# The last graph layer in eight units of 128 queries, its GpSimd operations as queued items of their own, and the folding of weights behind a step's piece

## The chip, the cores and the metric

The kernel runs on one core of a Trainium2 chip. The metric is the device time of one execution in microseconds (us), from runs on the chip; the profile of one execution gives start and length of every instruction on TensorE (PE, with its weight loads as PEld), VectorE (DVE), ScalarE (ACT), GpSimd (POOL) and the queue that issues most DMAs (SP).

## What is computed

Sixteen graphs of 1024 nodes with 128 features share one adjacency matrix. Three layers of masked attention with eight heads, each followed by a feed-forward network with layer norms, come first. Then comes one last layer of additive attention. Cut to what matters:

```python
# layers 0, 1, 2, for h [16, 1024, 128]; 8 heads of 16
scores = einsum('bnhd,bmhd->bhnm', Q, K) / sqrt(16)
scores = where(adj == 0, -inf, scores)
x = layer_norm(h + softmax(scores) @ V @ Wo + bo, ln1)
x = layer_norm(x + relu(x @ W1 + b1) @ W2 + b2, ln2)

# the last layer
h = x @ W
s_i = h @ a_src
s_j = h @ a_dst
e = s_i[:, :, None] + s_j[:, None, :]
e = where(e >= 0, e, 0.2 * e)
e = where(adj == 0, -inf, e)
y = softmax(e) @ h + x
return layer_norm(y, ln_gamma, ln_beta)
```

The kernel uses that exp(leaky(e)) is exp(0.2 s_i) exp(0.2 s_j) max(1, exp(0.8 (s_i + s_j))). The first factor cancels in the softmax, the second is multiplied into the node rows (`hd`), and what is left, max(1, product) times the 0/1 mask, is an outer product of two vectors of exponentials: that is what `edges` builds.

## The kernel before

**Blocks and steps.** A block m is one attention layer of one graph; there are 48. Four graphs ("lanes") go together: block order is layer 0 of graphs 0 to 3, layer 1 of graphs 0 to 3, layer 2 of them, and then the next four graphs. A block has 32 steps (g, qh, kt): two groups of four heads, two halves of 512 queries, eight tiles of 128 keys. So there are 1536 steps in a row, and n counts them. A half of a block here means the eight steps of one (g, qh).

**A step.** `score_step` (L532) issues four float32r matmuls of 512 columns (L540), the scores S of four heads, into two PSUM tiles from `slot()` (ring "s" of three). Of the first two heads, ACT takes the exponential (L548) and POOL multiplies by the 0/1 mask (L549); in eleven of the 32 steps (`BOTH_ON_DVE`), and always for the other two heads, DVE adds the mask (L552) and ACT takes the exponential after it (L564). The result is an `e_tile()`, from a ring of six. `av_due(n)` then issues the AV matmuls (L569) of the step four before (`AHEAD` = 4), which accumulate over eight steps; after the eighth DVE transposes the accumulator (L580) and POOL scales it (L584).

**Pieces.** All other work is cut into tasks that lie in chains. A task is (gap, function, tiles): it is due when its gap in steps since the chain's last task is over, and the tile words say which shared buffers it takes or frees. `piece()` (L863) runs after a step's AV and takes at most one due task without a star, and any number with a star. When a block ends its chains get the rest of its layer (attention output, feed-forward), and after layer 2 of a graph the tasks of the last layer, `last_tasks(b)` (L696). `need(mark)` forces a chain to its end at once if something later cannot start without it. A graph's x sits in one of five "x" tiles from its load until the task `store` frees it ("-x"); the load of graph b + 4's x needs such a tile, and its transpose by PE (L340) starts in the block ahead of its own.

**The last layer, for one graph.** xt(0) and xt(1) transpose x; xt(1) also lets POOL scale and shift x by the second layer norm of layer 2 (`scale_shift`, L440 and L441, 1024 elements wide). Three `nodes` tasks project (L378 with `w_nodes`) and take the exponentials. `rows_gh` and `send_rows` turn the two vectors of exponentials into rows and send them by 16 small DMAs to `g_rows` and `h_rows`, split into high and low parts, so that each edge matmul contracts four rows. Then four units u of 256 queries follow: `edges(u)` issues, for two slots, four float32r matmuls of 256 columns each (L772) in two row groups, and eight DVE operations of 128x256 that take the maximum with 1 and multiply by the mask (STT, L776) into an e tile; `aggregate(u)` issues the matmuls of that tile with `hd` (L378, tile `t<-hd,e`), then reciprocal (L789), scale and add x (L792), and statistics on DVE; after each second unit `normalise` runs on POOL (three small operations, then four at L436). `end` is four 512-wide operations on POOL by ln_gamma and ln_beta, and `store` eight DMAs (L811).

**Who orders what.** PE, ACT and SP execute in the order in which the program issues. DVE and POOL are ordered by a scheduler, by priority; `tc.issue_after(behind["pool"])` pins an instruction behind the newest mask multiply on POOL, and `soon()` raises a priority.

**Setup.** The dictionary `setup` (L316) holds, by step number, the loading and folding of later layers' weights (steps 8 to 82). Its matmuls (L273, L280, L291, L307) are issued ahead of the scores of their step:

```python
                now[0] = n
                if at == (6 if m == 0 else 1):
                    stack(m, 1)
                for run in setup.get(n, ()):
                    run()
```

Of the kernel before, what the change touches and what calls it, by code (L numbers as in the profile page):

```python
# [9 lines left out]
F32 = mybir.dt.float32  # L10
F32R = mybir.dt.float32r
BF16 = mybir.dt.bfloat16
# [6 lines left out]
P = 128  # L19
# [3 lines left out]
J = 4  # L23
# [96 lines left out]
def fast_path(ctx: ExitStack, tc: tile.TileContext, a: dict, out: bass.AP, flag):  # L120
# [28 lines left out]
        return work.tile([P, 512], F32, tag="w", name=name, bufs=TILES["w"])  # L149

    def e_tile():
        return work.tile([P, J, 512], F32, tag="e", name="e", bufs=6)


    def tokens(v):
# [36 lines left out]
    mask_add = const.tile([P, NT, N], F8W)  # L192
    rows_in = []
    for t in range(NT):
        if t < 6:
            ai = work.tile([P, 2, N], I32, tag="e", name="ai", bufs=6)
            ai, ab = ai[:, 0], ai.bitcast(BF16)[:, 1, :N]
        else:
# [497 lines left out]
    def last_tasks(b):  # L696
        s = {}
        g0 = 32 * (b % 2)

        def xt(h):  # L700
            def run():
                w = W[L - 1]
                if h == 0:

                    s["col"] = work.tile([P, 4, NT], F32, tag="col", name="col", bufs=2)
                    s["hd"] = [work.tile([P, 4, D + 1], F32, tag="w", name="hd", bufs=TILES["w"]) for _ in range(2)]
                    s["n"] = with_stats(state["x", b])
                s["xT", h] = half_tile("xT")
                transpose_half(s["xT", h], state["x", b], h, w["ln2_gc"], w["ln2_bc"])
                if h == 1:  # L710
                    scale_shift(state["x", b], w["ln2_g"], ln2_b_last)
            return run

        def nodes(t0, t1):
            def run():
                col, ts = s["col"], slice(t0, t1)

                halves = [slice(max(t0, 4 * h), min(t1, 4 * h + 4)) for h in range(2)]
                halves = [(c, s["hd"][c.start // 4][:, c.start % 4:(c.stop - 1) % 4 + 1, :])
                          for c in halves if c.start < c.stop]  # L720
# [36 lines left out]

        def edges(u):
            def run():
                e = s["e", u] = e_tile().rearrange("p j (c q) -> p (j c) q", q=256)  # L760
                half = slice(u // 2 * 512, u // 2 * 512 + 512)

                def queries(v):
                    return v.rearrange("p (j q) -> p j q", j=4)[..., u % 2 * 64:u % 2 * 64 + 64]

                for c in range(2):

                    ps = slot()
                    for i in range(2):
                        for r in range(2):  # L770
                            row = slice(64 * r + g0, 64 * r + g0 + 4)
                            nc.tensor.matmul(ps[:, (2 * r + i) * 256:(2 * r + i + 1) * 256],  # L772
                                             h_rows[row, (2 * i + c) * P:(2 * i + c + 1) * P],
                                             queries(g_rows[row, half]), start=True, stop=True)
                    for i in range(4):
                        nc.vector.scalar_tensor_tensor(e[:, c + 2 * i, :], ps[:, i * 256:(i + 1) * 256], 1.0,  # L776
                                                       queries(mask01[:, c + 2 * i, half]), op0=OP.max, op1=OP.mult)
            return run

        def aggregate(u):  # L780
            def run():
                e, ps = s["e", u], bank()
                for i in range(2):
                    for t in range(NT):
                        by_columns(ps[:, i * (D + 1):(i + 1) * (D + 1)],
                                   e[:, t, :].rearrange("p (j i e) -> p i j e", j=4, i=2)[:, i],
                                   s["hd"][t // 4][:, t % 4, :], start=(t == 0), stop=(t == NT - 1))
                pv = ps[:, :2 * (D + 1)].rearrange("p (i d) -> p i d", d=D + 1)
                nc.vector.reciprocal(s["col"][:, 3, 2 * u:2 * u + 2], pv[:, :, D])  # L789
                for i in range(2):  # L790
                    t = 2 * u + i
                    nc.vector.scalar_tensor_tensor(s["n"][0][:, t, :], pv[:, i, :D], s["col"][:, 3, t:t + 1],  # L792
                                                   state["x", b][:, t, :], op0=OP.mult, op1=OP.add)
                stats(s["n"], slice(2 * u, 2 * u + 2))
                if u % 2:
                    normalise(s["n"], slice(2 * u - 2, 2 * u + 2))
                if u == 3:
                    check_range(s["col"].rearrange("p c t -> p (c t)"))
            return run

        def end():
            y = s["n"][0]
            for h in range(2):
                scale_shift(y[:, 4 * h:4 * h + 4, :], wl["ln_gamma"], wl["ln_beta"])

        def store():
            y = s["n"][0]
            for h in range(2):
                queue = nc.scalar if h and b == B - 1 else nc.sync
                for j in range(4):  # L810
                    queue.dma_start(tokens(out[b])[j][:, h], y[j * SLOT:(j + 1) * SLOT, 4 * h:4 * h + 4, :])  # L811

        def two(f, g):
            def run():
                f()
                g()
            return run

        return [(5, xt(0), "+w +last +w +w"), (1, xt(1), "+w"), (2, nodes(0, 3), ""), (2, nodes(3, 6), ""), (2, nodes(6, 8), "-w -w"),
                (2, rows_gh, ""), (1, send_rows, "*"), (7, edges(0), ""), (3, two(edges(1), aggregate(0)), ""),  # L820
                (3, two(edges(2), aggregate(1)), ""), (3, two(edges(3), aggregate(2)), ""),
                (3, aggregate(3), ""), (4, end, "-last -w -w *"), (5, store, "-x *")]

    blocks = [(b, l) for p in range(0, B, LANES) for l in range(L) for b in range(p, p + LANES)]
# [121 lines left out]
    with tc.manual_schedule(engines={mybir.EngineType.PE, mybir.EngineType.Activation, mybir.EngineType.SP}):  # L949
        for m, (b, l) in enumerate(blocks):  # L950
# [284 lines left out]
```

## Time and profile before

| | |
|---|---|
| three runs | 3985.82, 3988.66, 3991.97 us; median 3988.66 |
| the profiled execution | 3988.0 us, its span 3985.9 us |
| mean granted TensorE clock | 0.975 |
| busy share of the span | PE 94%, DVE 87%, POOL 85%, ACT 83% |
| an ordinary block (3 to 8, 16 to 21, 28 to 33, 40 to 45 nearly all) | 70.9 us |
| blocks 10 to 15 | 82.2, 100.9, 100.3, 97.3, 96.1, 70.3 us |
| blocks 22 to 27 | 82.1, 101.1, 97.9, 96.8, 96.1, 70.4 us |
| blocks 34 to 39 | 82.7, 100.6, 100.3, 97.4, 96.0, 70.4 us |
| blocks 1 and 2 (weights are folded) | 73.5, 84.1 us |
| blocks 46 and 47 | 89.2, 99.6 us |
| from the end of block 47 to the end | 115 us |

A block's length is the time between the ends of its last accumulator transpose (L580) and that of the block before. The span runs from the first to the last instruction; the time of the execution holds 2.1 us more. In the windows below a line has the stretch, its length, then for each engine its busy time with the number of instructions, then the granted clock, the DMA engines' busy share and GB/s. A line of a timeline has start, length, engine, source line, operation, result<-operands, shape and count; in brackets the idle time ahead of it and what ended it. A line of waits has engine and waiting line, the line that it waited for, us in total, number of times and the longest. A line of groups has the busy total, the mean ns of one, and the idle time before. L378 and L340 are the lines of helpers, so these instructions are told apart by their tiles.

### The profile page before, as it was taken

How to read it: one execution, taken by the hardware profiler on the slowest of the kernel's cores; microseconds unless marked ns; L12 is line 12 of the kernel's file. 1: busy time of each engine (PE TensorE's matmuls, PEld its weight loads, DVE VectorE, ACT ScalarE, POOL GpSimd, SP SyncE). 2: the span in 40 equal slices, each digit the busy share in tenths (PEclk: the TensorE clock that was granted, in tenths of full speed). 3: DMA queues.
4: the chain of work that ended last, by engine and by line, in shares of the span. 5: the costliest groups of instructions: out<-in, count | busy, mean ns of one | idle time of the engine just before them, and what ended most of it. 6: DMA issues, size and time to landing. Idle time of an engine off the chain costs nothing.

```text
span 3985.9 us, 108397 instructions
## 1 busy us (share of the span) xinstructions
PE 3735.5 (94%) x43873; PEld 1501.6 (38%) x43873; DVE 3480.8 (87%) x5844; ACT 3289.4 (83%) x3797; POOL 3393.9 (85%) x2923
## 2 busy tenths in 40 slices
PE   7999999999999999998999999999999999999887
PEld 2333333344433333334444333333444433333346
DVE  6889999988889999998888999998888899999765
ACT  7989999977778999996776999998767799999750
POOL 4889999977789999997778999998778899999784
PEclk8999999999999999999999999999999999999998
DMA  5423424322223424332222423333222333324100
GB/s 139 114 65 92 100 71 111 80 66 65 66 66 87 111 69 104 84 90 67 62 67 68 112 67 102 88 85 98 66 55 66 86 75 99 94 73 115 49 7 20
DMA packets 245880, 319.19 MB, mean 80 GB/s; under 512 B 51072, under 2 KB 174208, under 8 KB 245376
## 3 DMA queue, kind: packets, MB, share of 16 engines
q1 hardware_dynamic: 243840, 311.52, 31.3%
q8 instruction: 349, 5.72, 0.6%
q14 instruction: 155, 1.27, 0.1%
q10 hardware_dynamic: 1536, 0.68, 0.1%
HBM read 58.53 MB, written 51.38 MB: 28 GB/s over the span
## 4 chain that ended last, share of the span: by engine, by line
PE 44%; DVE 23%; ACT 10%; POOL 8%; issue 6%; SPq 2%; DMA 1%; ACTq 0%; DVEq 0%; POOLq 0%
PE acc L569 16%; DVE e L552 16%; PE t L378 14%; PE s L540 11%; ACT e L564 5%; ACT e L548 3%; POOL e L549 2%; ACT hT L644 2%; POOL x L436 2%; PE s L378 1%; POOL x L440 1%; DVE st L408 1%; POOL x L441 1%; POOL mv L430 1%; DVE aT L598 1%
## 5 line engine op out<-in xcount | busy, mean ns | idle before, releaser
L552 DVE TENSOR_TENSOR e<-s,mask_add 128x1024 f32<-128x1024 f32 x2064 | 2410.6, 1209 | 166.7 <-PE s L540 133.6
L549 POOL TENSOR_TENSOR e<-e,mask 128x1024 f32<-128x1024 f32 x1008 | 2030.6, 2029 | 436.3 <-ACT e L548 435.5
L564 ACT ACTIVATE e<-e 128x1024 f32<-128x1024 f32 x2064 | 2145.0, 1061 | 190.6 <-DVE e L552 171.6
L569 PE MATMUL acc<-e,v 128*17 128x512 f32 x12288 | 1641.5, 606 | 52.2 <-POOL e L549 48.1
L540 PE MATMUL s<-Wq,Wk 64*128 64x512 f32 x6144 | 1237.7, 464 | 84.6 <-ACT e L548 29.8
L548 ACT ACTIVATE e<-s 128x1024 f32<-128x1024 f32 x1008 | 1032.2, 1024 | 311.7 <-PE s L540 311.0
L540 PEld LDWEIGHTS s<-Wq,Wk 64*128 64x128 f32 x6144 | 509.0, 186 | 1218.4 <-DVE e L552 492.6
L569 PEld LDWEIGHTS acc<-e,v 128*17 128x17 f32 x12288 | 205.6, 95 | 552.3 <-issue 418.4
L436 POOL TENSOR_SCALAR x<-x,mv 128x128 f32<-128x128 f32 x896 | 391.3, 453 | 19.2
L430 POOL TENSOR_TENSOR mv<-mv,half_neg 128x4 f32<-128x4 f32 (+1 forms) x179 | 214.3, 1197 | 14.7
L415 DVE TENSOR_TENSOR x<-t,x 128x512 f32<-128x512 f32 x191 | 132.0, 691 | 106.0 <-PE t L378 102.4
L378 PE MATMUL t<-x1T,W 128*32 128x512 f32 x1520 | 200.8, 600 | 5.1 <-DVE parts L743 3.2
L408 DVE BATCH_NORM_STATS2 st<-x 128x6 f32<-128x128 f32 x896 | 198.1, 281 | 6.3
L378 PEld LDWEIGHTS t<-W,hT 128*32 128x32 f32 x6080 | 173.8, 112 | 63.9 <-issue 57.0
L378 PE MATMUL t<-hd,e 128*32 128x129 f32 x6656 | 194.9, 274 | 3.0 <-DVE lo L468 3.0
L776 DVE SCALAR_TENSOR_TENSOR e<-s,mask 128x256 f32<-128x256 f32 x512 | 175.1, 411 | 22.0 <-PE s L772 21.9
L378 PE MATMUL t<-W,hT 128*32 128x128 f32 x6080 | 187.7, 276 | 2.9 <-DVE parts L743 2.9
L378 PEld LDWEIGHTS t<-hd,e 128*32 128x32 f32 x6656 | 182.1, 109 | 17.3 <-DVE lo L468 6.3
L580 DVE STREAM_TRANSPOSE tt<-acc 128x512 f32<-128x512 f32 x192 | 135.6, 706 | 36.2 <-PE acc L569 36.2
L644 ACT ACTIVATE hT<-t,b 128x512 f32<-128x512 f32 x190 | 131.0, 690 | 22.5 <-PE t L378 21.8
L510 POOL TENSOR_TENSOR x<-x,bo 128x1024 f32<-128x1024 f32 x48 | 114.9, 2393 | 9.7 <-PE s L378 7.2
L584 POOL TENSOR_TENSOR A<-tt,recs 128x256 f32<-128x256 f32 x192 | 120.3, 627 | 3.0 <-DVE recs L583 3.0
(141 smaller groups left out, 2450.1 us busy)
## 6 DMA issues: line engine op xcount, KB each, us to landing
Wk<-hi SPq DMA_DIRECT2D x384, 128.0 KB
Wk<-lo SPq DMA_DIRECT2D x384, 128.0 KB
Wq<-hi SPq DMA_DIRECT2D x384, 128.0 KB
Wq<-lo SPq DMA_DIRECT2D x384, 128.0 KB
tr<-xb SPq DMA_DIRECT2D x656, 64.0 KB
x1T<-tr SPq DMA_DIRECT2D x90, 256.0 KB
xT<-tr SPq DMA_DIRECT2D x74, 256.0 KB
x<-in_x_dram SPq DMA_DIRECT2D x124, 64.0 KB
```

The lines of the kernel that those rows point to most:

```text
L378: nc.tensor.matmul(dst[j:j + SLOT, :], cols, rhs, start=start, stop=stop)
L408: nc.vector.bn_stats(st[:, t, :], z[:, t, :])
L430: nc.gpsimd.tensor_tensor(v, v, half_neg[:, ts], OP.pow)
L436: nc.gpsimd.tensor_scalar(z[:, t, :], z[:, t, :], mv[:, t, 0:1], mv[:, t, 1:2], op0=OP.add, op1=OP.mult)
L540: nc.tensor.matmul(ps[:, r * 512:(r + 1) * 512], k[64 * r:64 * r + 64, kt * P:(kt + 1) * P], q[64 * r:64 * r + 64, q0:q0 + 512], start=Tru ...
L548: nc.scalar.activation(ev, psv, AF.Exp, scale=HD ** -0.5)
L549: behind["pool"] = nc.gpsimd.tensor_mul(ev, ev, m).ins
L552: behind["dve"] = nc.vector.tensor_add(ev, psv, m).ins
L564: nc.scalar.activation(ev, ev, AF.Exp, scale=HD ** -0.5)
L569: nc.tensor.matmul(acc[j * SLOT:j * SLOT + HD + 1, :], v_bufs[m % 2][:, kt, 2 * j + g, :], e[:, j, :], start=first, stop=last)
L644: nc.scalar.activation(s["h", f, h], ps, AF.Relu, bias=w["b1"][:, f:f + 1], scale=1.0)
L776: nc.vector.scalar_tensor_tensor(e[:, c + 2 * i, :], ps[:, i * 256:(i + 1) * 256], 1.0, queries(mask01[:, c + 2 * i, half]), op0=OP.max, o ...
```

## The change

The last layer is cut into eight units v of 128 queries. A unit takes one slot instead of two, eight matmuls of 128 columns instead of eight of 256, and four STT operations of 128x(8x32) elements instead of eight of 128x256; its edges lie in an `edge_tile`, from a ring of two of half the size of an e tile, for which the e ring goes from six to five. Tasks follow every two steps instead of three; the gaps of the last layer sum to 46 steps instead of 43. The row operations on POOL (ln2 on x, ln_gamma and ln_beta on the result) become tasks of one operation each, pinned behind the newest mask multiply, as is `normalise`. The result is stored in two halves at two times. `setup` runs after the step's piece instead of ahead of its scores. One of the tiles by which the adjacency matrix is loaded moves to the two edge tiles.

```diff
     def e_tile():
-        return work.tile([P, J, 512], F32, tag="e", name="e", bufs=6)
+        return work.tile([P, J, 512], F32, tag="e", name="e", bufs=5)
+
+    def edge_tile(dtype=F32):
+        return work.tile([P, N], dtype, tag="ee", name="ee", bufs=2)
...
-                if h == 1:
-                    scale_shift(state["x", b], w["ln2_g"], ln2_b_last)
...
+        def edges(v):
+            def run():
+                e = s["e", v] = edge_tile().rearrange("p (k q) -> p k q", q=P)
+                half, t = slice(v // 4 * 512, v // 4 * 512 + 512), v % 4 * SLOT
+                ps = slot()
+                for k in range(4):
+                    for r in range(2):
+                        row = slice(64 * r + g0, 64 * r + g0 + 4)
+                        nc.tensor.matmul(ps[:, r * 512 + k * P:r * 512 + (k + 1) * P], h_rows[row, k * P:(k + 1) * P],
+                                         g_rows[row, half].rearrange("p (j q) -> p j q", j=4)[:, :, t:t + SLOT],
+                                         start=True, stop=True)
+                for j in range(4):
+                    q = v // 4 * 512 + j * P + t
+                    nc.vector.scalar_tensor_tensor(e[:, :, j * SLOT:(j + 1) * SLOT],
+                                                   ps.rearrange("p (k q) -> p k q", q=P)[:, :, j * SLOT:(j + 1) * SLOT],
+                                                   1.0, mask01[:, :, q:q + SLOT], op0=OP.max, op1=OP.mult)
+            return run
...
+                stats(s["n"], slice(v, v + 1))
+                if v % 4 == 3:
+                    with tc.issue_after(behind["pool"]):
+                        normalise(s["n"], slice(v - 3, v + 1))
...
+        def by_rows(op, z, v, n=NT):
+            def run():
+                with tc.issue_after(behind["pool"]):
+                    op(z(), z(), rows(v(), n))
+            return run
...
-        return [(5, xt(0), "+w +last +w +w"), (1, xt(1), "+w"), (2, nodes(0, 3), ""), (2, nodes(3, 6), ""), (2, nodes(6, 8), "-w -w"),
-                (2, rows_gh, ""), (1, send_rows, "*"), (7, edges(0), ""), (3, two(edges(1), aggregate(0)), ""),
-                (3, two(edges(2), aggregate(1)), ""), (3, two(edges(3), aggregate(2)), ""),
-                (3, aggregate(3), ""), (4, end, "-last -w -w *"), (5, store, "-x *")]
...
+        mul, add = nc.gpsimd.tensor_mul, nc.gpsimd.tensor_add
+        tasks = [(5, xt(0), "+w +last +w +w"), (1, xt(1), "+w"), (2, nodes(0, 3), ""), (2, nodes(3, 6), ""),
+                 (0, by_rows(mul, x, lambda: W[L - 1]["ln2_g"]), "*"), (2, nodes(6, 8), "-w -w"),
+                 (0, by_rows(add, x, lambda: ln2_b_last), "*"), (2, rows_gh, ""), (1, send_rows, "*"), (7, edges(0), "")]
+        for v in range(NT - 1):
+            tasks.append((2, two(edges(v + 1), aggregate(v)), ""))
+            if v in (4, 6):
+                tasks.append((0, by_rows((mul, add)[v // 2 - 2], y(0), lambda v=v: wl[("ln_gamma", "ln_beta")[v // 2 - 2]], 4), "*"))
+        tasks += [(2, aggregate(NT - 1), ""), (2, store(0), "-last -w -w *"), (1, by_rows(mul, y(1), lambda: wl["ln_gamma"], 4), "*"),
+                  (2, by_rows(add, y(1), lambda: wl["ln_beta"], 4), "*"), (3, store(1), "-x *")]
+        return tasks
...
-                for run in setup.get(n, ()):
-                    run()
...
                 piece()
+                for run in setup.get(n, ()):
+                    run()
                 n += 1
```

More of the change, by code (lines that the diff above doesn't have):

```diff
@@ L194, in fast_path @@
     for t in range(NT):
-        if t < 6:
-            ai = work.tile([P, 2, N], I32, tag="e", name="ai", bufs=6)
+        if t < 5:
+            ai = work.tile([P, 2, N], I32, tag="e", name="ai", bufs=5)
             ai, ab = ai[:, 0], ai.bitcast(BF16)[:, 1, :N]
+        elif t == 5:
+            ai, ab = edge_tile(I32), edge_tile(I32).bitcast(BF16)[:, :N]
         else:
@@ L755, in send_rows @@
                                     parts[NT + 4 * r:NT + 4 * r + 4, i % 2, :].bitcast(F32))
-        def edges(u):
+        def edges(v):
             def run():
[L760 to L777, printed above, removed]
@@ L778, in edges, with aggregate @@
+                for j in range(4):
[3 more added lines that the diff above has]
+                                                   1.0, mask01[:, :, q:q + SLOT], op0=OP.max, op1=OP.mult)
             return run
-        def aggregate(u):
+        def aggregate(v):
             def run():
[L782 to L797, printed above, removed]
@@ new lines, in run @@
+                e, ps = s["e", v], bank()
+                for t in range(NT):
+                    by_columns(ps[:, :D + 1], e[:, t, :], s["hd"][t // 4][:, t % 4, :], start=(t == 0), stop=(t == NT - 1))
+                nc.vector.reciprocal(s["col"][:, 3, v:v + 1], ps[:, D:D + 1])
+                nc.vector.scalar_tensor_tensor(s["n"][0][:, v, :], ps[:, :D], s["col"][:, 3, v:v + 1],
+                                               state["x", b][:, v, :], op0=OP.mult, op1=OP.add)
+                stats(s["n"], slice(v, v + 1))
@@ L798, in run @@
+                if v % 4 == 3:
+                    with tc.issue_after(behind["pool"]):
+                        normalise(s["n"], slice(v - 3, v + 1))
+                if v == NT - 1:
                     check_range(s["col"].rearrange("p c t -> p (c t)"))
             return run
[L801 to L808, printed above, removed]
+        def by_rows(op, z, v, n=NT):
[3 more added lines that the diff above has]
+            return run
@@ L809, in store, with x, y @@
+        def x():
+            return state["x", b]
+        def y(h):
+            return lambda: s["n"][0][:, 4 * h:4 * h + 4, :]
+        def store(h):
+            def run():
+                y = s["n"][0]
                 queue = nc.scalar if h and b == B - 1 else nc.sync
```

## The prediction

> **What bounds the kernel now.** I read the clock and span per core first (one core, span 3985.9 us, mean clock 0.975, run 3988.0), then the page's engine shares (PE 94%, DVE 87%, POOL 85%, ACT 83%), then the ends of the 48 blocks from the accumulator transposes (L580). Most blocks take 70.9 us. Blocks 10 to 14 take 82.2, 100.9, 100.3, 97.3 and 96.1, and so do 22 to 26 and 34 to 38. There the last layer of four graphs is threaded through the attention steps. The windows of block 8, of block 11 and of block 11's third half:
>
> ```profile
> 624.90:695.70 70.80, 69.05 (x712) 24.16 (x708) 66.38 (x100) 66.81 (x75) 65.83 (x55) 1.00 0.36 92
> 849.20:950.10 100.90, 91.88 (x1331) 43.26 (x1325) 82.93 (x165) 71.02 (x88) 79.12 (x73) 0.96 0.26 62
> 902.70:929.50 26.80, 20.57 (x185) 6.25 (x177) 17.69 (x22) 18.79 (x32) 24.54 (x18) 0.87 0.55 122
> ```
>
> Columns: length, then busy us (instructions) of PE, PEld, DVE, ACT, POOL, then clock, DMA share, GB/s. An ordinary block is PE's. Block 11 has 9 us of idle PE, most of it in the third half, where POOL is busy 24.54 of 26.80 and the clock drops. The waits of blocks 11 to 14 name it, and the slots:
>
> ```profile
> PEld acc L569 <- POOL e L549: 17.7, 14, 4.8
> PE acc L569 <- POOL e L549: 12.3, 5, 4.3
> PEld s L540 <- DVE e L776: 5.6, 7, 1.5
> ```
>
> POOL's and PE's timelines show one such stall:
>
> ```profile
> 905.03 1.29 POOL L440 TENSOR_TENSOR x<-x,ln_gamma 128x512 f32<-128x512 f32 x1
> 906.40 1.29 POOL L441 TENSOR_TENSOR x<-x,ln_beta 128x512 f32<-128x512 f32 x1
> 907.65 2.01 POOL L549 TENSOR_TENSOR e<-e,mask 128x1024 f32<-128x1024 f32 x1
> 909.62 2.38 POOL L440 TENSOR_TENSOR x<-x,ln_g 128x1024 f32<-128x1024 f32 x1
> 912.08 2.36 POOL L441 TENSOR_TENSOR x<-x,ln_b_last 128x1024 f32<-128x1024 f32 x1
> 914.39 2.00 POOL L549 TENSOR_TENSOR e<-e,mask 128x1024 f32<-128x1024 f32 x1
> ...
> 911.37 0.73 PE L540 MATMUL s<-Wq,Wk 64*128 64x512 f32 x4
> 916.45 1.91 PE L569 MATMUL acc<-e,v 128*17 128x512 f32 x8 [4.35 <-POOL e L549]
> ```
>
> The mask multiply waits behind two 1024-wide row operations; AV waits 4.35 us for it and then takes 1.91 us instead of 1.05. A unit of the last layer on PE, and its groups in block 11:
>
> ```profile
> 864.96 1.10 PE L772 MATMUL s<-g_rows,h_rows 4*128 4x256 f32 x8
> 865.99 3.76 PE L378 MATMUL t<-hd,e 128*32 128x129 f32 x128
> ...
> L378 PE MATMUL t<-hd,e 128*32 128x129 f32 x512 | 15.0, 274 | 0.0
> L776 DVE SCALAR_TENSOR_TENSOR e<-s,mask 128x256 f32<-128x256 f32 x32 | 10.9, 411 | 0.0
> ```
>
> Weight folding and the x load stall PE as well:
>
> ```profile
> 197.31 0.33 PE L273 MATMUL t<-identf,w_nodes 128*128 128x128 f32 x1 [1.47 <-ACT v L479]
> 203.76 0.38 PE L280 MATMUL t<-a,w3t 128*128 128x2 f32 x2 [1.95 <-DVE lo L468]
> 1152.98 0.63 PE L340 MATMUL t<-identf,x 128*128 128x128 f32 x4 [2.42 <-DMA x<-in_x_dram]
> ```
>
> [...] edge matmuls run as pairs in two row groups, and pairs start 0.224 us apart[...]. [...] The trace has float32r at 512 columns (pairs 0.337 us apart) and 256 (0.224)[...], none at 128. [...] The changed STTs read runs of 32; no trace here shows that shape. [...]
>
> **The excess that can go.** Blocks 10 to 15 take 547.3 us (767.0 to 1314.3) against 6 x 70.9 = 425.4: 121.9 us too much for four graphs. PE work of one last layer, from the groups of that window by shape: aggregate 15.0, edges 3.5, nodes 2.3, transposes 1.3, rows 0.3, together 22.4; four are 89.6. So 32.3 us are waiting and half clock.
>
> **Part 1, single POOL items.** Removed: `scale_shift` inside xt(1) and the pair in `end`. Added: the same four operations as tasks pinned behind the newest mask multiply, and normalise pinned likewise. Total POOL work is equal; its place changes. In block 11, between the masks of steps 14 and 19, POOL has 25.3 us of items before; by the program's new order it has 19.2, against five steps x 2.2 = 11 us plus the PE work threaded in (about 8). So POOL still fills the stretch but no pair of 2.4 us stands ahead of one mask. I let all 32.3 us go here except what part 3 makes.
>
> **Part 2, eight units.** Per graph 64 edge matmuls of 128 columns for 32 of 256. [...] A unit of 4 pairs is then 0.68, eight are 5.4 against 4 x 0.9 = 3.6 (units measured 0.68 to 1.10): +1.8 per graph, +7.3 per four. Aggregation has the same matmuls. DVE: 32 STTs of 256 elements as before, at 411 ns (nothing below, as the elements are the same[...]); 8 reciprocals for 4 (+0.17 each, +0.7 per graph). The pace is now one unit each two steps instead of three. Two steps then cost PE 2 x 1.53 (scores 0.66, AV 0.87, start to start) + 0.95 (projection and post pieces) + 0.68 + 1.88 (half an aggregate) = 6.6 us, DVE 2.69 adds (11 of 32 steps have two, the others one) x 1.21 + 4 x 0.41 + 1.0 (reciprocal, x STT, statistics) + 1.2 of others = 7.1, some 6.9 after overlap of starts. DVE passes PE by 0.3; seven such pairs in four graphs are 8, of which I take 5, since steps between have slack. Bounds 0 and 30 (were every pair to lose 1 us). A second benefit, one PSUM slot per unit instead of two, removes the 5.6 us of L540 waits for L776; it is inside the 32.3. The ring of e falls from 6 to 5 tiles with AHEAD 4: the score of a step reuses the tile whose AV was issued just before it, so it waits only where AV itself is late. No stall is priced; if one shows, it is up to 0.5 us in the 26 or so heavy steps of a block.
>
> **Part 3, the chain's length and SP.** The gaps of a chain sum to 46 steps for 43. With five x tiles, the third graph of a group is still in its chain when its tile is wanted; then the program forces the chain out at step 0 of block 14 (26, 38), and the out stores stand directly ahead of the x loads in SP's queue, where before the row transfers lay between. Chain: score, exp, mask, normalise 3.3, two row operations 2.6, about 9.6 us; 4 stores issue in 2.4, eight x loads in 3.8, and the landings (1.3 us each, from the load issued from 1147.94 to 1151.7 and used at 1152.98) bring it to 18 or 19 us. PE reaches the transpose of x at some 11: a wait near 8 where 2.42 stands now, +5.6, perhaps a halved clock after it: +6.3 per group. Bounds: 0 (transfers overlap) to 20.
>
> **Part 4, folding behind the piece.** The matmuls are the same 5.3 us; but they now stand after the step's AV and piece, when the results they need are ready. The waits of blocks 1 and 2 sum to 9.8 (in block 2: 1.47, 1.95, 1.44, 0.81, 0.81, 1.77; about 1.5 in block 1). I take 8 off. The DMA issues of `setup` move only past one piece's issues.
>
> **Part 5, blocks 46 and 47, and the tail.** They take 89.2 and 99.6, 47 above ordinary. With the same share of waiting as above (32.3/121.9) that is 12.4; less the edges' 1.8 and DVE's 1.3 for each of two graphs: -6. In the tail, row transfers expose 7.40 + 0.48 us before and stay; 4 units take 23.2 us, eight at 2.75 + 2.3 to finish take 24.3, but the first store starts earlier: -2.
>
> **Sum.** Per group -32.3 + 6.3 + 7.3 + 5 = -13.7; three groups -41; folding -8; end -8: -57. On the run of 3988.0 that is 3931; the median, 3988.7, is the same run to 0.02%. I say 3930.
>
> **Rivals.**
> R1, slower: [...] Pairs are 0.33, a unit +0.64 us, 16 x 8 units +82: 4012. For it: no trace here has that width, and the kernel before had none under 256. [...] It decides from 57/128/4 = 0.11 us above 0.17, so pairs of 0.28.
> R2: VectorE becomes the bound. The two-step pairs lose 0.3 + 1 us each, 28 a group less 5: some 12 us more in each group, 3965. For it: 82.93 of 100.9 busy in block 11 already; against: PE is still the longer in the ordinary steps between.
> R3: the forced chain. If the stall of part 3 is 26 to 30 us instead of 6.3, that is three times 20 to 24: 3990 to 4002. For it: SP's order and the doubled length of the chain ahead of it; against: the load of 1147.94 had landed at 1152.98, 1.3 us after its last issue ended, so a transfer itself is short.
>
> **Chances.** Forecast 54%, R1 22%, R2 13%, R3 11%. The likeliest's own range is 3890 (no forced wait, -19; no DVE loss, -15; a few us of the tail) to 3960. The whole range, 3890 to 4005, takes in R2, R3 and leaves out most of R1. A measurement tells 0.2%, 8 us. Faster: 0.54 + 0.11 + 0.02 + 0.02 = 0.69; same 0.06; slower 0.19 + 0.06 = 0.25.
>
> **What would show it.** In the changed trace: edge pairs 0.17 apart (R1: 0.33); the STT group near 411 ns; L549's waits under 10 us in blocks 11 to 14, those blocks near 92 to 96; the x wait of block 14 near 8; blocks 1 and 2 shorter by 8 in all. Wrong would be block lengths unchanged while POOL's waits are gone: then DVE has taken over.

## The result and the profile after

The changed kernel takes 3939.14 us (median of four runs, 3936.96 to 3943.14); the kernel before took 3987.36 us beside it. The ratio is 0.988 with a 95% interval of 0.9864 to 0.9896: 48 us, or 1.2%, faster, where 3930 was forecast. The profiled run has a span of 3935.1 us for 3985.9, and its clock is 0.982 for 0.975.

Where the 50.8 us between the two spans come from. A block is counted here to the start of its last accumulator transpose, which lies 0.7 us ahead of that transpose's end:

| stretch | before | after | difference | forecast |
|---|---|---|---|---|
| blocks 0 to 3 | 341.3 | 335.4 | -5.9 | -8 |
| blocks 10 to 15 | 547.3 | 533.0 | -14.3 | -13.7 |
| blocks 22 to 27 | 544.4 | 533.5 | -10.9 | -13.7 |
| blocks 34 to 39 | 547.3 | 533.4 | -13.9 | -13.7 |
| blocks 46 and 47 | 188.7 | 184.4 | -4.3 | -6 |
| behind block 47 | 114.9 | 112.3 | -2.6 | -2 |

The other blocks are 1.1 us longer in sum. The page has one group whose idle time tells most of the story, the AV matmuls (busy us, mean ns, then idle time before them and what ended it). Before:

```profile
L569 PE MATMUL acc<-e,v 128*17 128x512 f32 x12288 | 1641.5, 606 | 52.2 <-POOL e L549 48.1 <-DVE tt L580 3.6
```

And after, where the lines of the code are five further down:

```profile
L574 PE MATMUL acc<-e,v 128*17 128x512 f32 x12288 | 1628.2, 602 | 12.7 <-POOL e L554 9.3
```

PE waited 48.1 us in front of AV for the mask multiplies on POOL, and now waits 9.3. In blocks 10 to 15 alone it was 13.8 us, and is 2.3 (a line of waits, before and after):

```profile
PE acc L569 <- POOL e L549: 13.8, 6, 4.3
PE acc L574 <- POOL e L554: 2.3, 3, 1.3
```

The windows of block 8, of block 11 and of block 11's third half (length, busy us of PE, PEld, DVE, ACT, POOL, clock, DMA share, GB/s), after:

```profile
619.10:690.00 70.90, 69.18 (x712) 24.29 (x707) 66.39 (x100) 66.92 (x75) 65.78 (x55) 1.00 0.38 93
844.20:933.90 89.70, 88.25 (x1285) 40.94 (x1281) 81.15 (x157) 69.60 (x88) 76.61 (x73) 1.00 0.23 59
896.10:916.40 20.30, 19.79 (x194) 6.43 (x192) 17.46 (x21) 19.05 (x31) 20.19 (x16) 1.00 0.58 143
```

Block 11 has 1.45 us of idle PE where it had 9, and the clock is full. In its third half POOL is still busy for practically the whole time (20.19 of 20.30): what went is not POOL's load. POOL's timeline shows what did:

```profile
900.14 2.04 POOL L554 TENSOR_TENSOR e<-e,mask 128x1024 f32<-128x1024 f32 x1
902.13 1.30 POOL L798 TENSOR_TENSOR x<-x,ln_gamma 128x512 f32<-128x512 f32 x1
...
903.96 2.03 POOL L554 TENSOR_TENSOR e<-e,mask 128x1024 f32<-128x1024 f32 x1
905.93 1.30 POOL L798 TENSOR_TENSOR x<-x,ln_beta 128x512 f32<-128x512 f32 x1
907.17 2.04 POOL L554 TENSOR_TENSOR e<-e,mask 128x1024 f32<-128x1024 f32 x1
...
915.82 2.38 POOL L798 TENSOR_TENSOR x<-x,ln_g 128x1024 f32<-128x1024 f32 x1
918.28 2.40 POOL L798 TENSOR_TENSOR x<-x,ln_b_last 128x1024 f32<-128x1024 f32 x1
920.64 2.01 POOL L554 TENSOR_TENSOR e<-e,mask 128x1024 f32<-128x1024 f32 x1
```

The masks stand between the row operations. But the pair of 1024-wide operations still stands in one piece ahead of a mask (915.82 and 918.28), and no AV waits for it. The waits of blocks 11 to 14 (engine and line, what it waited for, total, times, longest):

```profile
PE t L345 <- DMA x<-in_x_dram: 6.9, 1, 6.9
...
PEld acc L574 <- POOL e L554: 3.9, 11, 0.4
```

Before, the two lines for POOL were 17.7 and 12.3. The first line is the x load behind the forced chain: SP issues it only from 1123.40 us on, behind the last stores of the graph that had to give up its tile. A unit on PE and the groups of block 11 after:

```profile
853.62 0.66 PE L769 MATMUL s<-g_rows,h_rows 4*128 4x128 f32 x8
854.21 1.98 PE L383 MATMUL t<-hd,ee 128*32 128x129 f32 x64
856.12 0.73 PE L545 MATMUL s<-Wq,Wk 64*128 64x512 f32 x4
...
L774 DVE SCALAR_TENSOR_TENSOR ee<-s,mask 128x256 f32<-128x256 f32 x24 | 8.4, 413 | 0.0
```

From the start of a unit's edges to the next matmul are 0.59 us (853.62 to 854.21), and 1.91 us for its aggregate. The folding and the x load:

```profile
195.17 0.33 PE L278 MATMUL t<-identf,w_nodes 128*128 128x128 f32 x1
201.48 0.35 PE L285 MATMUL t<-a,w3t 128*128 128x2 f32 x2 [1.69 <-DVE lo L473]
...
1128.19 1.09 PE L345 MATMUL t<-identf,x 128*128 128x128 f32 x4 [6.93 <-DMA x<-in_x_dram]
```

The wait of 1.47 us in front of the first folding matmul is gone; the second, 1.95 before, is still 1.69. But a wait has come up that was not there. In blocks 1 and 2 PE's waits for DVE in front of the scores (first line before, second after) sum to 3.3 us for 0.4:

```profile
PE s L540 <- DVE e L552: 0.4, 1, 0.4
PE s L545 <- DVE e L557: 3.3, 3, 2.7
222.79 0.50 PE L545 MATMUL s<-Wq,Wk 64*128 64x512 f32 x2 [2.71 <-DVE e L557]
```

The scores wait there for a mask addition on DVE, which starts at 221.52 us, behind 4.2 us of folding work on DVE (217.40 to 221.6).

To see what PE spends on each kind of work, I added up, in blocks 10 to 15, the time from the start of each group of matmuls to the start of the next (so a wait counts to the group ahead of it):

| | six ordinary blocks | before | after |
|---|---|---|---|
| scores S, with the wait behind them | 153.4 | 159.9 | 141.8 |
| AV, with the wait behind them | 179.2 | 194.5 | 194.2 |
| projections and feed-forward | 92.7 | 96.0 | 93.9 |
| aggregates | | 58.9 | 61.0 |
| edges | | 20.0 | 23.7 |
| nodes, transposes, rows | | 18.0 | 18.4 |
| sum | 425.3 | 547.3 | 533.0 |

The gain is behind the scores, where AV waits for its mask: 18.1 us. Of these, 11.5 are the waits for POOL shown above (13.8 to 2.3); the rest, half clock (a granted 0.50 for 34.1 us of these blocks before and for 17.1 after) and shorter waits, was not taken apart. The scores even cost less than in ordinary blocks. There PE's waits for ACT and DVE in front of the scores sum to 9.2 us in six blocks, here to 3.1; that the other work in each step makes the difference is likely, but was not tested.

### The profile page after: what moved, and what is told of

Its sections match the earlier page's. It is cut to its first block, busy times and chain, and to the rows that moved or that the text cites. A ratio compares the mean times of both kernels' runs of the same rounds, so it can differ in the third digit from the quotient of the medians.

```text
span 3935.1 us, 109752 instructions
## 1 busy us (share of the span) xinstructions
PE 3742.7 (95%) x44385; PEld 1519.1 (39%) x44385; DVE 3512.1 (89%) x5908; ACT 3289.2 (84%) x3797; POOL 3386.4 (86%) x2923
## 4 chain that ended last, share of the span: by engine, by line
PE 50%; DVE 22%; ACT 11%; issue 6%; POOL 5%; DMA 3%; SPq 3%; DVEq 0%; ACTq 0%; POOLq 0%
PE acc L574 18%; DVE e L557 15%; PE t L383 15%; PE s L545 13%; ACT e L569 5%; ACT e L553 3%; POOL e L554 2%; PE s L769 2%; ACT hT L649 2%; PE s L383 1%; DMA x1T<-tr 1%; DVE st L413 1%; POOL x L441 1%; DVE xb L357 1%; DVE aT L603 1%
## 5 line engine op out<-in xcount | busy, mean ns | idle before, releaser
L553 ACT ACTIVATE e<-s 128x1024 f32<-128x1024 f32 x1008 | 1031.9, 1024 | 294.1 <-PE s L545 279.5
L774 DVE SCALAR_TENSOR_TENSOR ee<-s,mask 128x256 f32<-128x256 f32 x512 | 179.5, 412 | 32.4 <-PE s L769 32.4
L383 PE MATMUL t<-hd,ee 128*32 128x129 f32 x6656 | 205.7, 274 | 2.7 <-DVE x L420 2.7
L383 PEld LDWEIGHTS t<-hd,ee 128*32 128x32 f32 x6656 | 178.8, 109 | 16.4 <-DVE x L420 5.3
```

What stands on the lines that cost most here:

```text
L383: nc.tensor.matmul(dst[j:j + SLOT, :], cols, rhs, start=start, stop=stop)
L553: nc.scalar.activation(ev, psv, AF.Exp, scale=HD ** -0.5)
L774: nc.vector.scalar_tensor_tensor(e[:, :, j * SLOT:(j + 1) * SLOT], ps.rearrange("p (k q) -> p k q", q=P)[:, :, j * SLOT:(j + 1) * SLOT], 1 ...
```

## The experiments

Twelve kernels were run, in three groups of four, each beside the kernel before (its median is 3987.1, 3985.3 and 3985.7 us in the three). The ratio is to that kernel, with its interval; differences to the changed kernel are between medians, 3939.14 us for it.

**Run 1: the folding alone.** The kernel before with

```diff
-                for run in setup.get(n, ()):
-                    run()
...
                 piece()
+                for run in setup.get(n, ()):
+                    run()
                 n += 1
```

> The kernel before with one edit alone: setup runs after the step's piece. Theory (the waits in front of the folding matmuls go, the rest of the change has nothing to do with it): 5 to 8 us off the kernel before, all of it in blocks 1 and 2, blocks 10 to 15 within 1 us of before. Rival (the shorter blocks 1 and 2 of the changed kernel come from somewhere else, or the folding moves its wait to the next step): within 2 us of before.

Measured: 3982.16 us, ratio 0.9987 (0.998 to 0.9993). Block 3 ends at 334.9 us for 341.3; the stretches of heavy blocks are 0.6 to 3.2 us longer (blocks 10 to 15 by 1.6, where at most 1 was expected). So the folding is worth 5 us by itself. The rival is right in part: the trace has the same new wait of the scores for DVE (2.69 us at 222.24). Whether the gain is independent of the rest is not shown: in run 3, where the folding stands as before, blocks 0 to 3 are 3.3 us shorter as well, for a reason that was not looked for.

**Run 2: the POOL part alone.** The kernel before with its four units of 256 queries (the gaps sum to 43 steps, not to the 42 of the expectation), and

```diff
-                if h == 1:
-                    scale_shift(state["x", b], w["ln2_g"], ln2_b_last)
...
-                if u % 2:
-                    normalise(s["n"], slice(2 * u - 2, 2 * u + 2))
+                if u % 2:
+                    with tc.issue_after(behind["pool"]):
+                        normalise(s["n"], slice(2 * u - 2, 2 * u + 2))
...
+                (0, by_rows(mul, x, lambda: W[L - 1]["ln2_g"]), "*"), (2, nodes(6, 8), "-w -w"),
+                (0, by_rows(add, x, lambda: ln2_b_last), "*"), (2, rows_gh, ""), (1, send_rows, "*"), (7, edges(0), ""),
```

> The kernel before with only the POOL part: four units of 256 queries stay, the row operations become single queued tasks, normalise is pinned, the store goes in two halves; the gaps sum to 42 steps. Theory A (the mask multiplies waiting behind pairs of row operations are the excess): blocks 10 to 15 lose 25 us or more a group, as no edge matmul is added and no chain is forced; total 3895 to 3915, below the changed kernel. Rival B (the smaller units, with one PSUM slot each and a more even pace, are what removes the waits): blocks 10 to 15 lose under 8 us a group, total 3965 to 3987.

**Run 3: the units alone.** The changed kernel with the POOL part and `setup` as before.

```diff
+                if h == 1:
+                    scale_shift(state["x", b], w["ln2_g"], ln2_b_last)
...
-                    with tc.issue_after(behind["pool"]):
-                        normalise(s["n"], slice(v - 3, v + 1))
+                    normalise(s["n"], slice(v - 3, v + 1))
...
+        return tasks + [(2, aggregate(NT - 1), ""), (4, end, "-last -w -w *"), (4, store, "-x *")]
```

> The changed kernel with its POOL part and its setup put back as before: eight units of 128 queries and edge tiles, row operations in pairs inside xt(1) and end, normalise not pinned. Theory A: the POOL waits of before stay, the added edge and aggregate starts (about 5 us a group) and the forced chain (about 6) come on top: 4010 to 4025. Rival B: most of the gain is here: 3940 to 3960.

Measured: run 2 takes 3947.66 us, ratio 0.9908 (0.9895 to 0.9922); run 3 takes 3948.32, ratio 0.9906 (0.9891 to 0.9921). Neither theory holds for both: run 2 lies between the two ranges, and run 3 in that of B. Each half alone gives 39 us; with run 1 that would be 83 us if they added up, and together they give 48. Blocks 10 to 15 take 530.3 us in run 2 and 536.1 in run 3, both against 547.3. The changed kernel takes 533.0 there, which is 2.7 us more than the POOL part alone. In the profiled executions its lead over run 2 comes from elsewhere: the first four blocks (4.5 us, the folding) and the end from block 46 on (296.7 us for 307.5).

**Run 4: the late x.** The changed kernel with

```diff
-AT = {"xP": (4, 6), "proj": (5, 7, 9, 11, 17, 19), "post": (13, 15, 17, 18, 21, 22, 22, 23, 24, 25, 27, 29, 31, 35, 38, 40)}
+AT = {"xP": (7, 8), "proj": (5, 7, 9, 11, 17, 19), "post": (13, 15, 17, 18, 21, 22, 22, 23, 24, 25, 27, 29, 31, 35, 38, 40)}
...
-            put(([(6, scale, "*")] if l else []) + [(2 if l else 6, shift, "*")], ("shifted", m))
+            put(([(6, scale, "*")] if l else []) + [(2 if l else 10, shift, "*")], ("shifted", m))
```

> The changed kernel with the transposes of a late x at steps 7 and 8 of its block instead of 4 and 6, and the bias added to x at step 10 instead of 6. Theory (the 6.9 us wait for x in blocks 14, 26 and 38 is the price of the forced chain and has nothing else behind it): the wait is gone, 15 to 21 us off the changed kernel, 3918 to 3925. Rival (the wait only moves, since the projections, the stack or POOL come up against the late x): under 5 us off, 3934 or more.

Measured: 3921.34 us, ratio 0.9842 (0.9828 to 0.9855), 17.8 us below the changed kernel. The x wait is gone from the trace and blocks 10 to 15 take 527.3 us for 533.0. The theory holds in its number: the wait behind the forced chain costs some 6 us a group. It is not true that nothing else hangs on it. In block 14 four masks now start 8.5 to 9.1 us after their exponentials, and AV's waits for POOL in blocks 10 to 15 are 5.5 us for 2.3.

**Runs 5 and 6: which edit on POOL.** As either half was enough, I suspected a coincidence of two pieces of POOL work that any spreading breaks. Run 5 is the kernel before with x's scale and shift moved out of xt(1), unpinned; run 6 is run 2 without any pin.

```diff
-                if h == 1:
-                    scale_shift(state["x", b], w["ln2_g"], ln2_b_last)
...
+                (0, lambda: scale_shift(state["x", b], W[L - 1]["ln2_g"], ln2_b_last), "*"), (2, nodes(6, 8), "-w -w"),
```

> The kernel before with one edit alone: the scale and shift of x (two 1024-wide operations on POOL, still together and not pinned) leave xt(1) and become a task five steps later. Theory C (the excess is one coincidence, the end of one graph's last layer on POOL meeting the next graph's x operations, so any edit that spreads the two apart gives most of the gain; that is why either half of the change alone gave 39 us): 20 to 40 us off the kernel before, 3947 to 3967. Rival A (it takes the splitting into single operations or the pins): under 10 us off, 3977 or more.

```diff
-                with tc.issue_after(behind["pool"]):
-                    op(z(), z(), rows(v(), n))
+                op(z(), z(), rows(v(), n))
```

> The POOL part alone on the kernel before, as in the run of that part, but with no operation pinned behind the newest mask multiply. Theory C (what counts is where the tasks stand): within 8 us of that run, 3940 to 3956. Rival A (the pins keep the row operations from going ahead of masks): 15 us or more slower than it, 3962 to 3987.

Measured: run 5 takes 3989.14 us, ratio 1.0006 (0.9998 to 1.0014), run 6 takes 3991.02, ratio 1.0014 (1.0007 to 1.002). My theory fell: neither edit gains anything, and run 6 is even 5.8 us slower than the kernel before, outside both ranges of its expectation. POOL's timeline of run 6 at the same place shows why:

```profile
907.84 2.01 POOL L549 TENSOR_TENSOR e<-e,mask 128x1024 f32<-128x1024 f32 x1
909.81 2.38 POOL L801 TENSOR_TENSOR x<-x,ln_g 128x1024 f32<-128x1024 f32 x1
912.27 2.35 POOL L801 TENSOR_TENSOR x<-x,ln_b_last 128x1024 f32<-128x1024 f32 x1
914.59 1.99 POOL L549 TENSOR_TENSOR e<-e,mask 128x1024 f32<-128x1024 f32 x1
```

Although they are single tasks some steps later in the program, the operations stand where they stood before, to 0.2 us. POOL's order is the scheduler's, and without a pin it puts them in the same places.

**Run 7: is DVE level with PE?** The changed kernel with the last STT of each unit issued twice.

```diff
-                for j in range(4):
+                for j in (0, 1, 2, 3, 3):
```

> The changed kernel with the last of a unit's four STT operations issued twice, 0.41 us more of DVE per unit, 128 units. Theory of the prediction (DVE is level with PE in the pairs of steps of the heavy stretches): a good part of 128 x 0.41 = 53 us appears, 30 us or more, 3969 or later. Rival (DVE still has slack there, as the trace of the changed kernel shows no PE wait for it beyond 0.5 us): under 12 us, 3951 or earlier.

Measured: 3961.70 us, ratio 0.9939 (0.9926 to 0.9953), 22.6 us above the changed kernel; 128 units of 0.412 us are 52.7 us. Both numbers of the expectation are missed: 43% of the added DVE time shows. The windows of blocks 10 to 15, first the changed kernel, then run 7:

```profile
761.00:1294.00 533.00, 509.91 (x6855) 227.63 (x6848) 473.19 (x874) 417.80 (x503) 449.47 (x401) 0.98 0.30 76
```

```profile
763.00:1303.60 540.60, 512.13 (x6857) 227.64 (x6852) 484.54 (x905) 418.16 (x503) 449.75 (x401) 0.98 0.30 75
```

DVE has 11.35 us more and the stretch is 7.6 longer, two thirds of it; the last four graphs, at the end of the kernel, have 13.2 us more of DVE and are 3.2 longer. DVE is neither free nor the bound: it is late in some of the steps.

**Run 8: an earlier chain.** Run 4 with the chain begun after 3 steps for 5.

```diff
-        tasks = [(5, xt(0), "+w +last +w +w"), (1, xt(1), "+w"), (2, nodes(0, 3), ""), (2, nodes(3, 6), ""),
+        tasks = [(3, xt(0), "+w +last +w +w"), (1, xt(1), "+w"), (2, nodes(0, 3), ""), (2, nodes(3, 6), ""),
```

> The changed kernel with the late transposes of x, and the last layer's chain begun 3 steps after its predecessor's last task instead of 5. Theory (in the first graph of each group the row transfers then stand ahead of the 16 stacking transfers in SP's queue, and the 4.0 us wait for h_rows goes): 8 to 13 us below the run with the late x alone, 3908 to 3914. Rival (the wait is the transfers' own length, or the earlier start makes PE wait for POOL's normalised x): within 4 us of that run, 3917 to 3925.

Measured: 3924.38 us, ratio 0.9841 (0.9828 to 0.9855), no better than run 4. The wait for h_rows is gone, as the theory has it, but the stacking transfers now stand behind the rows and are late in their turn:

```profile
836.12 0.79 PE L545 MATMUL s<-Wq,Wk 64*128 64x512 f32 x2 [5.37 <-DMA tr<-xb]
```

The transfer named there is none that this matmul reads. It reads the stacked Wq and Wk, whose transfers are the last ones that SP issues ahead of it:

```profile
831.63 1.23 SPq L530 DMA_DIRECT2D Wq<-lo  x2
832.97 2.35 SPq L361 DMA_DIRECT2D tr<-xb  x4
```

That it was these is inferred from the operands and from SP's order. SP issues rows and stack for 22.7 us together (810.19 to 832.86). In run 4 the rows went second and were waited for (4.5 us), here it is the stack.

**Runs 9 and 10: pins without splitting, splitting undone.** After runs 5 and 6 the theory was that only pins move work on POOL, and that a mask may be late by a certain time before anything waits. Run 9 is the kernel before with the three pins and nothing else (the ones at `normalise` and `end` like the first):

```diff
                 if h == 1:
-                    scale_shift(state["x", b], w["ln2_g"], ln2_b_last)
+                    with tc.issue_after(behind["pool"]):
+                        scale_shift(state["x", b], w["ln2_g"], ln2_b_last)
```

> The kernel before with nothing but the pins: normalise of the last layer, the scale and shift of x in xt(1) and the four operations of end are each tied behind the newest mask multiply; tasks, pairs and gaps stay. Theory D (only the pins move work on POOL, splitting does nothing by itself): the gain of the POOL part returns, 3940 to 3962. Rival (a pair pinned in one place is as long an obstacle as before): 3975 or more.

Run 10 is the changed kernel with scale and shift together again in each task:

```diff
+        def pair(z, g, c, n=NT):
+            def run():
+                with tc.issue_after(behind["pool"]):
+                    scale_shift(z(), g(), c())
+            return run
```

> The changed kernel with each scale and its shift back together in one task (x: 2 x 1024 wide; the result: 2 x 512 wide, in each half), still pinned. Theory of the threshold (a mask multiply may start some 8.5 us after its exponential before AV, four steps behind, waits for it; the changed kernel's latest starts 6.9 us after, so 2.4 us more are hidden): within 6 us of the changed kernel, 3933 to 3945. Rival (single items are what counts): 10 us slower or more, 3949 or later.

Measured: run 9 takes 3955.86 us, ratio 0.9923 (0.991 to 0.9937): 30 us from three pins. Run 10 takes 3939.11 us, ratio 0.9884 (0.9869 to 0.9899), the same as the changed kernel. POOL's timeline of run 9:

```profile
902.70 2.02 POOL L549 TENSOR_TENSOR e<-e,mask 128x1024 f32<-128x1024 f32 x1
904.68 2.40 POOL L440 TENSOR_TENSOR x<-x,ln_g 128x1024 f32<-128x1024 f32 x1
907.15 2.40 POOL L441 TENSOR_TENSOR x<-x,ln_b_last 128x1024 f32<-128x1024 f32 x1
909.52 2.00 POOL L549 TENSOR_TENSOR e<-e,mask 128x1024 f32<-128x1024 f32 x1
...
914.05 2.52 POOL L440 TENSOR_TENSOR x<-x,ln_gamma 128x512 f32<-128x512 f32 x2
916.53 2.52 POOL L441 TENSOR_TENSOR x<-x,ln_beta 128x512 f32<-128x512 f32 x2
```

The pair for x is as long as ever. But the operations of `end`, two of which stood right in front of the first of these masks, have moved behind two more masks. Nothing else has changed its order at this place, so it looks to be the pin at `end` that counts here; the three pins were not tried one by one. In the changed kernel the splitting into single items does nothing (run 10). With four units, run 2 is 8 us faster than run 9; the intervals of the two overlap, and whether the splitting or the new places of the tasks bring these 8 us was not tried.

**Run 11: POOL work added.** The changed kernel with two multiplications of x by a row of ones (`unit`) right behind the shift of x:

```diff
                     op(z(), z(), rows(v(), n))
+                    for _ in range(2 if op == add and n == NT else 0):
+                        nc.gpsimd.tensor_mul(z(), z(), rows(unit, n))
```

> The changed kernel with two more 1024-wide multiplications of x by ones on POOL right behind the shift of x, 4.8 us of POOL per graph, 77 us in all. Theory of the threshold (5.7 + 4.8 = 10.5 us of delay, over the 8.5 to 9 us that four steps cover): 2 to 5 us a graph, 3955 to 4000. Rival 1 (POOL has room, nothing shows): under 3948. Rival 2 (POOL is the bound of the stretch, all 77 us show): 4005 or later.

Measured: 3978.07 us, ratio 0.9977 (0.9967 to 0.9986), 38.9 above the changed kernel, 2.4 us a graph where 4.8 of POOL were added. For each kernel I took, in blocks 10 to 15, the time from the end of a mask's exponential on ACT to the start of its multiply on POOL (126 masks). The last column is PE's line in the view of the waits of these blocks:

| kernel | median us | largest delay | over 6 us | over 8 us | AV starts within 0.3 us of its mask's end | PE waits for POOL in front of AV, us |
|---|---|---|---|---|---|---|
| before | 3987.4 | 11.7 | 20 | 12 | 7 | 13.8 |
| run 6, split, not pinned | 3991.0 | 11.7 | 20 | 12 | 7 | 13.5 |
| run 9, pins only | 3955.9 | 9.8 | 14 | 4 | 8 | 8.1 |
| run 3, units only | 3948.3 | 8.8 | 16 | 3 | 8 | 6.7 |
| run 2, POOL part only | 3947.7 | 6.1 | 1 | 0 | 0 | none |
| changed | 3939.1 | 6.9 | 5 | 0 | 5 | 2.3 |
| run 10, pairs pinned | 3939.1 | 7.0 | 6 | 0 | 5 | 2.7 |
| run 11, more POOL work | 3978.1 | 10.0 | 25 | 8 | 15 | 15.7 |
| run 4, late x | 3921.3 | 9.1 | 9 | 4 | 9 | 5.5 |

AV comes four steps behind its scores. In the kernel before, a mask that was 1.4 us late (step 14 of block 11) ended 8.1 us ahead of its AV, one that was 7.3 us late (step 18) ended 0.1 us ahead of it, and the next, 11.5 us late, is the stall of 4.35 us. So a delay is free up to a limit and what is above is paid, and behind this stall half clock came on top (the AV behind the 4.35 us took 1.91 us at a granted clock of 0.50, for 1.05 at 1.00). The limit is not one number: in the changed kernel AV starts right behind masks that were 5.7 to 6.9 us late, while in run 3 a mask 8.1 us late (step 4 of block 14) ended 7.7 us ahead of its AV. That would follow if the limit is the time that PE spends and waits in the four steps; it was not tested. The last column says why the halves don't add: there were 13.8 us of such waits a group, of which run 2 alone takes away all and run 3 alone 7.1, so the second half finds little left. Run 4 is the reminder that this is one cost among several: its masks are later than the changed kernel's, and it is faster, since its wait for x is gone.

**Run 12: the rows by ACT.** Run 4, with half of the row transfers of each group's first graph issued by ACT:

```diff
-                queue = nc.scalar if r and b == B - 1 else nc.sync
+                queue = nc.scalar if r and (b == B - 1 or b % LANES == 0) else nc.sync
```

> The changed kernel with the late transposes of x, and in the first graph of each group eight of the 16 row transfers issued by ACT instead of SP. Theory (the rows wait on SP's issue time of 0.65 us each, and ACT's exponentials can be 5 us late as the masks can): the 4.5 us wait for h_rows goes, 9 to 14 us below the run with the late x alone, 3907 to 3913. Rival (ACT pays for the issues what SP saves): within 4 us of that run.

Measured: 3911.64 us, ratio 0.9813 (0.98 to 0.9827), 9.7 us below run 4: the fastest kernel here, 27.5 us below the changed one. The price is visible on ACT:

```profile
819.90 0.60 ACTq L757 DMA_DIRECT2D h_rows<-parts  x1
820.55 2.00 ACT L569 ACTIVATE e<-e 128x1024 f32<-128x1024 f32 x2 [4.58 <-DMA g_rows<-parts]
```

ACT's exponentials stand still for 4.58 us while it issues, and this is hidden only in part. The scores that come next wait 2.87 us for ACT, and the AV behind them takes 1.91 us for 1.05:

```profile
823.51 1.22 PE L545 MATMUL s<-Wq,Wk 64*128 64x512 f32 x4 [2.87 <-ACT e L553]
824.66 1.91 PE L574 MATMUL acc<-e,v 128*17 128x512 f32 x8
```

What is gained is the difference: blocks 10 to 15 take 524.9 us for 527.3 in run 4.

## Why the prediction was right, and where its reasons were not

**Part 1, POOL.** The forecast let 32.3 us a group go, with 6.3 us back for the forced chain and 5 for DVE: -21.0. Behind the scores, AV and the projections the traces show -20.5 (-18.1, -0.3, -2.1). The sum is right, by some luck; its cause is not as stated. The 32.3 us set the blocks' length against busy time. Counted from start to start as in the table above, the blocks held 25.1 us more than ordinary blocks and the last layer's work, and hold 4.6 after the change. "No pair of 2.4 us stands ahead of one mask" is not what helps: a pair stands there after the change too, and run 10 shows that pairs cost nothing there. The new place of the tasks does nothing by itself (runs 5 and 6). The pins do it (run 9), and so do the smaller units (run 3), which the forecast had mainly as a cost. At the place of the long stall, POOL's row operations come in run 3 in the order of before, but three masks instead of one stand between `end` and the pair for x:

```profile
902.41 1.29 POOL L446 TENSOR_TENSOR x<-x,ln_beta 128x512 f32<-128x512 f32 x1
903.65 4.01 POOL L554 TENSOR_TENSOR e<-e,mask 128x1024 f32<-128x1024 f32 x2
...
908.20 2.02 POOL L554 TENSOR_TENSOR e<-e,mask 128x1024 f32<-128x1024 f32 x1
910.18 2.38 POOL L445 TENSOR_TENSOR x<-x,ln_g 128x1024 f32<-128x1024 f32 x1
```

Which property of the units does it, the even pace, the single slot or the shorter bursts on DVE, was not tried. The benefit of the single slot came as forecast: the waits of scores for a slot held by the edges, 3.1 us in blocks 10 to 15 before and in run 2, are gone in the changed kernel and in run 3.

**Part 2, units.** The edges were put at +7.3 us a group; they are +3.7. A unit takes 0.59 us (the median of all units too) instead of the forecast's 0.68, since pairs start 0.16 us apart once and 0.11 twice, for the 0.17 taken. The 0.17 was an estimate; a line through the measured 0.337 us at 512 columns and 0.224 at 256 gives it. Not priced was a cost of cutting the aggregate in two: 1.91 us for each half against 3.68 for the whole, +2.1 a group, and +0.4 for nodes. Together +6.2. DVE at 5 us, with bounds of 0 and 30, cannot be read off by itself; run 7 shows that it is late for part of the time, as assumed. The STT takes 413 ns in runs of 32 for 411 before.

**Part 3, the forced chain.** A wait near 8 us was forecast where 2.42 stood, and 6.93 came. The mechanism was right. The forecast's 18.9 us for three groups were for what comes on top of the 2.42; measured by the waits that is 4.5 a group, 13.5 in all. The 17.8 us of run 4 are what taking away the whole wait brings, the 2.42 included and the later masks deducted.

**Part 4, folding.** -8 was taken of 9.8. The trace has -5.9, run 1 -5.0. The waits of the folding matmuls themselves did go nearly as forecast, from 10.0 us to 2.3. What the forecast left out is DVE: the folding's work there now stands ahead of a mask addition, and 2.9 us come back as a wait of the scores (2.7 of them at one place, in run 1 as well). And results "are ready" was not true everywhere: the second matmul still waits 1.69 us, as it did 1.95.

**Part 5, the end.** -8 was forecast, -6.9 came. The rows' wait in the tail, 7.40 + 0.48 us before, which "stays", has moved. For graph 15 it is 0.55 + 0.48 now, as units of graph 14 lie ahead of it; but graph 14's own rows, which were not waited for before, now are:

```profile
3870.06 1.08 PE L769 MATMUL s<-g_rows,h_rows 4*128 4x128 f32 x7 [5.13 <-DMA h_rows<-parts]
```

So 7.9 us became 6.2.

**Rivals.** R1 assumed 0.33 us per pair, nearly the 0.337 measured at 512 columns, and so 1.3 per unit; measured is 0.59. R2 is half there: added DVE time shows at 43%. Its own sum does not come out: 28 pairs of steps that lose 1.3 us each, less the 5 already counted, are 31 us a group and not 12, which would have put R2 near 4020. R3 fell with the 6.93 us.

## What to carry to other kernels

Where work is issued several steps ahead of its use, a delay costs nothing up to a limit, which differs from place to place (here a mask 5.7 us late was already up against its AV, and one 8.1 us late still 7.7 us ahead of it); measure how late each producer is against that limit, and price an edit by what it takes off the peaks above it, not by the work it moves. Two edits that lowered the same peak did not add up here (39 us each, 48 together), so try each alone before giving either the credit. On an engine that a scheduler orders, the place of an instruction in the program is only a wish (in run 6 tasks moved by some steps stood in the old places, to 0.2 us): look at the order in the trace, and pin what has to stay behind something.

## What the runs showed of the hardware that had not been expected

Pairs of 128-column matmuls in two row groups start 0.16, 0.11 and 0.11 us apart within a unit, less than the 0.17 us forecast from the first spacing alone; the medians of the three spacings at 256 columns, in the kernel before, are 0.223, 0.120 and 0.125. In the unit shown above, the weight loads of the second pair begin 0.107 us after the start of the first, those of the third and fourth only 0.05 us after the start of the pair ahead. An aggregate of 64 records costs 0.07 us more than half of one of 128 (1.91 against 1.84). And a stretch with more TensorE work per step had less waiting behind the scores than an ordinary one, 141.8 against 153.4 us for 192 steps.
